# Another order for the query tasks in two steps around layer 1 of a two-layer attention kernel

## The chip, the cores and the metric

One core of a Trainium2 chip runs the whole kernel. The metric is the device time of one launch in microseconds (us). The kernel before takes 2398.43 us, the median of three runs from 2395.92 to 2399.86.

## The reference

The input x is 8 images of 32 x 32 points with 256 channels in 32-bit floats, so 1024 tokens per image. Two layers follow each other.

```python
# layer 0: attention with 4 heads, C = 256 channels per head
qkv = einsum('bnc,cd->bnd', xf, W_qkv)          # q, k, v
atten = softmax(einsum('bihd,bjhd->bijh', q, k) * C ** -0.5, axis=2)
res = einsum('bijh,bjhd->bihd', atten, v).reshape(B, -1, h * C)
x = einsum('bnd,dc->bnc', res, W_out) + b_out + xf
# layer 1: attention with one head, keys and queries of 32 channels
f, g, h = x @ Wf + bf, x @ Wg + bg, x @ Wh + bh
o = einsum('bij,bjd->bid', softmax(einsum('bik,bjk->bij', g, f)), h)
y = gamma * o + x
```

## The kernel before

**Steps.** The work is cut into units and steps. A unit is one head of layer 0 for one image (class `Layer0`) or layer 1 for one image (class `Layer1`). Each unit has two steps, one for each block of 512 of its 1024 query tokens. The list `steps` runs over the images. For every image after the first, layer 1 of the image before is put between its heads 1 and 2, for the last image behind head 3 (`behind`). Layer 1 of the last image comes at the very end. So layer 1 stands between two heads of layer 0 six times.

**What one step holds.** The loop that ends at the edit writes the order out by hand. In it `a` and `blk` are the unit and block of step i, `one` and `two` are the steps one and two before, and `nxt` is the next. A step computes the scores of its own block, the product of the probabilities of `one` with the values, and the output projection of `two`; in the last step of a unit also the queries of the next unit. Each task gets a place, a number, with `put`; the tasks of a step are emitted in the order of these numbers. TensorE, VectorE and ScalarE are scheduled by hand (`manual_schedule`), so this is the order in which these three engines run. A number has no unit; only the order counts.

**Tasks of layer 0.** Its scores, its products and its queries use a scheme with seven block products in place of eight (`seven`, L222). A call makes three tasks and holds three PSUM banks, x, y and z. Task one (L254) writes the three banks; ScalarE copies x to SBUF as e, and VectorE adds y and e to u. Task two (L261) adds products onto x and y; then ScalarE takes x out, and VectorE adds y and e to v and z and v to an output. Task three (L268) adds products onto y and z, and VectorE makes the last two outputs, which frees these banks. Scores make two such calls per step, six tasks, placed at 0, 2, 4, 6, 8 and 10 (L815). Queries and products make one call each. A call for the product has three tasks, of which the third is put into the next step (L823). The scheme needs sums and differences of its operands, on VectorE: four small ones of the queries (`qsums`, L460, L461), four of the probabilities (L526, L529), called s1 to s4 in the order of their making, and per image those of the values and keys.

**Tasks of layer 1.** A scores task (L647) computes four 128 x 512 pieces, each into a PSUM bank of its own. A matmul here uses 32 of the 128 rows, and four lie side by side. ScalarE copies the banks to SBUF (L660). VectorE takes the maximum (L697 to L703), GpSimd makes it one over all partitions (L705), VectorE subtracts (L712) and ScalarE exponentiates (L717), a quarter of the block at a time. A block's product is four tasks (L726), each with a bank of its own for 16 matmuls (each 32-bit float matmul is two in the profile), and VectorE normalises and adds (L738, L740).

**Buffers.** The pool `ps` has six PSUM banks, shared by the scores, the products and the queries. Two more (`psm`) serve projections and transposes.

**The places around the change.** The queries and their sums are placed at L841 to L845:

```python
if is_l0(nxt) and blk == NBLK - 1:
    queries, qsums = nxt[0].queries()
    put(queries, *((1.5, 2.5, 4.5) if not l0 or is_l0(two) else (0.5, 1.5, 4.5)))
    put(qsums, *((5.4, 6.4, 7.2, 7.4) if l0 else (6.7, 6.9, 7.3, 7.6)))
```

In layer 1's second step the scores tasks are at 0.5 and 2 (L818), the softmax pieces at 0.9, 2.7, 4.2, 5, 6.2, 6.8 and 7.5, the products at 1, 4, 6 and 8 (L835) and the projections at 3 and 7 (L825). In a layer 0 step the product of `one` has its two tasks at 5 and 9 (L833), with its sums at 2.2, 3.2, 4.2 and 5.2 (L830, L831). The case `(0.5, 1.5, 4.5)` is a step of layer 0 with no layer 0 step two before it: head 2's second block behind layer 1, six times, and step 1 of the whole run.

Of the kernel before, what the change touches and what calls it, by code (L numbers as in the profile page):

```python
# [20 lines left out]
def kernel(  # L21
# [93 lines left out]
    def load_x(b, parts=1):  # L115
        t = tile_of("rows", [P, NT, C], f"x_{b}")
        n = HT // parts
        for k in range(NBLK):
            for i in range(parts):
                nc.sync.dma_start(  # L120
                    t[:, k * HT + i * n : k * HT + (i + 1) * n, :].rearrange("p t c -> p (t c)"),
                    x_v[b][:, k, ts(i, n * C)],
                )
        rows[b] = t
# [206 lines left out]
    def transpose_rows(b, src, dst, layer):  # L331


        def task(k, c):
            if b not in dst:
                dst[b] = tile_of("xT", [P, CC, N], f"x{layer}T_{b}")
            pt = tile_of("psm", [P, NB], f"px{layer}_{b}_{k}_{c}")
            for t in range(HT):
                nc.tensor.transpose(  # L339
                    pt[:, ts(t, P)], src[b][:, k * HT + t, ts(c, P)], ident  # L340
                )
            nc.scalar.copy(dst[b][:, c, ts(k, NB)], pt)

        return [partial(task, k, c) for k in range(NBLK) for c in range(CC)]

    def key_sums(b):

        made = {}

        def piece(i):  # L350
            if i == 0:
                xT = xT_of[b]
                t = tile_of("v", [P, 4, HN], f"xs_{b}")
                sums = [t[:, k, :] for k in range(4)]
                blocks = [xT[:, c, ts(k, HN)] for k in range(2) for c in range(CC)]
                made["l"] = sum_a(sums, *blocks)
                xblocks[b] = a_operands(blocks, sums)
            made["l"][i]()

        return [partial(piece, i) for i in range(4)]  # L360

    def value_sums(b):

        made = {}

        def piece(i):
            if i == 0:
                r = rows[b]
                t = tile_of("xt", [P, 4, NT // 2, P], f"xt_{b}")
                blocks = [r[:, ts(j, NT // 2), ts(c, P)] for j in range(2) for c in range(CC)]  # L370
                sums = [t[:, k] for k in range(4)]
                made["l"] = sum_b(sums, *blocks)
                vblocks[b] = b_operands(blocks, sums)
            made["l"][i]()

        return [partial(piece, i) for i in range(4)]

    def residual(b):


        def piece(i):
            if i == 0:
                rows1[b] = tile_of("rows", [P, NT, C], f"x1_{b}")
            nc.vector.tensor_tensor(
                rows1[b][:, ts(i, 2), :], rows[b][:, ts(i, 2), :],
                bout_sb.unsqueeze(1).broadcast_to([P, 2, C]), ALU.add,
            )

        return [partial(piece, i) for i in range(NT // 2)]
# [387 lines left out]
    def behind(b):  # L777

        return 2 if b < B - 1 else HEADS
# [10 lines left out]
    queries, qsums = first.queries()  # L790
# [5 lines left out]
    def is_l0(s):  # L796
        return s is not None and isinstance(s[0], Layer0)

    def step(k):
        return steps[k] if 0 <= k < len(steps) else None  # L800
# [4 lines left out]
    for i, (a, blk) in enumerate(steps):  # L805
        l0 = isinstance(a, Layer0)
        one, two, nxt = step(i - 1), step(i - 2), step(i + 1)
        places = []

        def put(tasks, *at):  # L810
            assert len(tasks) == len(at)
            places.extend(zip(at, range(len(places), len(places) + len(at)), tasks))

        if l0:
            put(a.scores(blk), 0, 2, 4, 6, 8, 10)  # L815
        else:
            tasks, pieces = a.scores(blk)
            put(tasks, *((0.5, 2.4) if blk == 0 else (0.5, 2)))  # L818
            put(pieces, *((1.6, 3.9, 6.2, 6.5, 7.4, 8.4, 8.6) if blk == 0 else
                          (0.9, 2.7, 4.2, 5, 6.2, 6.8, 7.5)))  # L820
        if is_l0(two):
            u, k = two
            put(u.products_of[k][2:], 1 if l0 else 0)  # L823
            put([partial(u.invert, k)], 2.9 if l0 or blk == 1 else 1.9)
            put(u.project(k), *((3, 7) if l0 else (2, 6) if blk == 0 else (3, 7)))  # L825
        if is_l0(one):
            u, k = one
            sums, keys = u.sums(k)
            u.products_of[k] = u.products(k)
            put(sums[:2] + sums[3:], *((2.2, 3.2, 4.2) if l0 else (0.8, 2.2, 4.5)))  # L830
            put(sums[2:3], 5.2 if l0 else 5.5)  # L831
            put(keys, *((6.2, 8.2) if l0 else (7.6, 9.6)))
            put(u.products_of[k][:2], *((5, 9) if l0 else (4, 7)))  # L833
        elif one is not None:
            put(one[0].products(one[1]), *((3, 5, 7, 9) if l0 else (1, 4, 6, 8)))  # L835
        if i == 0:
            fold = fold_weights(1) + fold_weights(2) + fold_weights(3)
            put(fold, -2, -1, *[0.9 + 0.6 * n for n in range(len(fold) - 2)])
        if i == 1:
            put([partial(nc.vector.tensor_scalar, bh_sb, bh_sb, gamma_sb, None, ALU.mult)], 8.5)  # L840

        if is_l0(nxt) and blk == NBLK - 1:
            queries, qsums = nxt[0].queries()
            put(queries, *((1.5, 2.5, 4.5) if not l0 or is_l0(two) else (0.5, 1.5, 4.5)))
            put(qsums, *((5.4, 6.4, 7.2, 7.4) if l0 else (6.7, 6.9, 7.3, 7.6)))  # L845

        if l0 and a.h == 0 and blk == 0:
            put(residual(a.b), 5.3, 6.3, 7.3, 7.4)
        if l0 and a.h == 0 and blk == 1:
            put(value_sums(a.b), 1.4, 2.4, 3.4, 4.4)  # L850
        if l0 and a.h == 2 and blk == 0 and a.b + 1 < B:
            load_x(a.b + 1)
        if l0 and a.h == HEADS - 1 and blk == 0 and a.b + 1 < B:
            put(transpose_rows(a.b + 1, rows, xT_of, 0), 1.5, 2.5, 3.5, 4.5)
            put(key_sums(a.b + 1), 5.4, 6.4, 7.2, 7.4)

        if l0 and a.b > 0 and a.h == behind(a.b) - 1:
            if blk == 0:
                put(transpose_rows(a.b - 1, rows1, x1T_of, 1), 2.5, 4.5, 6.5, 8.5)
            else:  # L860
                put(nxt[0].queries(), 1.4, 1.5, 3.5)
        if not l0 and blk == 0:
            put(a.values(), 0.9, 1, 3, 5, 8)
        if nxt is None:
            put(transpose_rows(B - 1, rows1, x1T_of, 1), 8.1, 8.2, 8.3, 8.4)
            put(final.queries(), 9, 9.1, 9.3)
        for _, _, t in sorted(places, key=lambda x: x[:2]):
            t()
# [136 lines left out]
```

## Time and profile before

| | before |
|---|---|
| time, median of 3 (us) | 2398.43 |
| span of the profiled execution (us) | 2399.1 |
| instructions | 25946 |
| DVE busy (us) | 1584.2 |
| ACT busy (us) | 623.7 |
| POOL busy (us) | 236.5 |
| mean granted TensorE clock | 0.997 |

PE is TensorE's matmuls, PEld its weight loads, DVE is VectorE, ACT is ScalarE, POOL is GpSimd. Times in rows are microseconds if not marked ns. A row of the waits reads: engine, what it wrote and the line, `<-` what released it, then the total time in us, how often, and the longest. A row of the timeline reads: start from the beginning of the span, duration, engine, line, operation, output `<-` inputs, how many were merged, and in brackets the idle time before it with its releaser. Ends of matmuls are modelled, starts are recorded. A row of the windows gives the busy time of PE, PEld, DVE, ACT and POOL, then the granted clock as a share of full speed, the DMA share and GB/s. Of the names: psx, psy and psz are banks of layer 0's scores, with `_q` of the queries, with `_y` of the products; ps_l and pa_l are banks of layer 1's scores and products; po is a projection's.

### The profile page before, as it was taken

The page shows a single profiled execution, that of the slowest core. Times are in us where ns is not written, and L with a number is a line of the kernel's source. Part 1 is how long each engine was busy: PE and PEld are TensorE (multiplying, and loading weights), DVE is VectorE, ACT ScalarE, POOL GpSimd, SP SyncE. Part 2 cuts the span into 40 slices and gives each one's busy share as a digit, 9 for nine tenths or more (in the row PEclk, how much of TensorE's full clock was granted, in tenths as well). Part 3 has the DMA queues.
Part 4 walks back from the last instruction along what each step waited for, and adds up shares of the span by engine and source line. Part 5 has one row for each costly group of instructions (what it writes and reads, how often), then busy time and mean ns, then how long its engine had stood idle before and what let it go on. Part 6 is the DMA issues. An engine that isn't in the chain of part 4 may idle for free.

```text
span 2399.1 us, 25946 instructions
## 1 busy us (share of the span) xinstructions
PE 2373.5 (99%) x10608; PEld 1951.4 (81%) x10608; DVE 1584.2 (66%) x2477; ACT 623.7 (26%) x1001; POOL 236.5 (10%) x93
## 2 busy tenths in 40 slices
PE   8999999999999999999999999999999999999999
PEld 6888888788877888788887888878888788888877
DVE  5666777567675676666766667666676666766665
ACT  2222223222232222322223222222222322222232
POOL 0111111011110111101111011110111100011110
PEclk9999999999999999999999999999999999999999
DMA  3000000000000000000000000000000000000000
GB/s 117 1 1 1 1 18 1 18 1 12 7 1 18 1 19 1 1 18 1 18 1 1 18 1 18 1 1 18 1 18 1 1 18 1 1 1 1 1 10 28
DMA packets 43536, 23.63 MB, mean 10 GB/s; under 512 B 36049, under 2 KB 38097, under 8 KB 43409
## 3 DMA queue, kind: packets, MB, share of 16 engines
q1 hardware_dynamic: 43408, 21.90, 3.2%
q8 instruction: 85, 1.39, 0.2%
q14 instruction: 43, 0.34, 0.0%
HBM read 13.37 MB, written 8.52 MB: 9 GB/s over the span
## 4 chain that ended last, share of the span: by engine, by line
PE 96%; DVE 3%; ACT 0%; DMA 0%; issue 0%; SPq 0%; DVEq 0%; ACTq 0%
PE psy L235 14%; PE psy_y L235 13%; PE po L586 9%; PE pa_l L730 9%; PE psx_y L235 9%; PE psz L235 9%; PE psx L235 9%; PE psz_y L235 9%; PE psy_q L235 4%; PE psx_q L235 2%; PE psz_q L235 2%; PE pr_v_l L419 2%; PE ps_l L651 1%; PE px L339 1%; PE pm_fg L399 1%; DVE s_l L712 1%
## 5 line engine op out<-in xcount | busy, mean ns | idle before, releaser
L542 POOL PARTITION_ALL_REDUCE rb<-rs x64 | 206.9, 3233 | 1903.3 <-DVE rs L540 1903.3
L235 PE MATMUL psy<-qs,xs 128*128 128x256 f32 x1024 | 262.9, 379 | 1.3 <-DVE qs L461 1.3
L490 ACT ACTIVATE p<-p 128x1024 f32<-128x1024 f32 x128 | 135.3, 1057 | 492.7 <-DVE p L252 492.7
L235 PE MATMUL psx<-q,x0T 128*128 128x256 f32 x1024 | 262.8, 379 | 0.0
L235 PE MATMUL psz<-q,xs 128*128 128x256 f32 x1024 | 262.8, 379 | 0.0
L586 PE MATMUL po<-wvo,y 128*128 128x256 f32 x1024 | 242.6, 380 | 0.0
L235 PE MATMUL psx_y<-p,x 128*128 128x256 f32 x1024 | 242.0, 379 | 0.0
L235 PE MATMUL psy_y<-s,xt 128*128 128x256 f32 x1024 | 241.9, 379 | 0.0
L730 PE MATMUL pa_l<-v_l,s_l 128*128 128x257 f32 x1024 | 231.7, 381 | 2.3 <-DVE y L252 1.9
L235 PEld LDWEIGHTS psx<-q,x0T 128*128 128x128 f32 x1024 | 193.9, 190 | 39.7 <-issue 15.3
L730 PEld LDWEIGHTS pa_l<-v_l,s_l 128*128 128x128 f32 x1024 | 193.7, 190 | 39.0 <-issue 12.6
L586 PEld LDWEIGHTS po<-wvo,y 128*128 128x128 f32 x1024 | 193.7, 191 | 38.1 <-issue 13.9
L235 PEld LDWEIGHTS psx_y<-p,x 128*128 128x128 f32 x1024 | 192.9, 190 | 36.0 <-issue 12.0
L235 PEld LDWEIGHTS psy<-qs,xs 128*128 128x128 f32 x1024 | 194.5, 190 | 28.1 <-DVE qs L461 1.7
L235 PEld LDWEIGHTS psz<-q,xs 128*128 128x128 f32 x1024 | 194.6, 190 | 26.4
L235 PEld LDWEIGHTS psy_y<-s,xt 128*128 128x128 f32 x1024 | 193.8, 190 | 27.2
L252 DVE TENSOR_TENSOR u<-psy,e 128x512 f32<-128x512 f32 x128 | 88.5, 691 | 155.5 <-PE psy L235 81.1
L264 ACT ACTIVATE p<-psx 128x512 f32<-128x512 f32 x128 | 76.4, 597 | 373.6 <-PE psx L235 373.4
L252 DVE TENSOR_TENSOR v<-psy,e 128x512 f32<-128x512 f32 x128 | 88.1, 688 | 103.4 <-PE psy L235 103.1
L235 PE MATMUL psy<-qs,x0T 128*128 128x256 f32 x512 | 132.1, 380 | 5.5 <-DVE v L252 5.5
L597 DVE SCALAR_TENSOR_TENSOR x<-po,inverse,x 128x256 f32<-128x256 f32 x256 | 111.9, 478 | 25.3 <-PE po L586 15.3
L258 ACT COPY e<-psx 128x512 f32<-128x512 f32 x128 | 73.8, 577 | 206.4 <-PE psx L235 206.4
(108 smaller groups left out, 3164.8 us busy)
## 6 DMA issues: line engine op xcount, KB each, us to landing
out_dram<-x SPq DMA_DIRECT2D x15, 512.0 KB, 2.6
x<-in_x_dram SPq DMA_DIRECT2D x14, 512.0 KB, 4.3
w<-in_L_conv_W_qkv_dram SPq DMA_DIRECT2D x4, 768.0 KB
x<-in_x_dram SPq DMA_DIRECT2D x4, 256.0 KB, 4.5
w<-in_L_conv_W_out_dram SPq DMA_DIRECT2D x4, 256.0 KB, 9.3
line<-rb SPq DMA_DIRECT2D x64, 2.0 KB
st<-line SPq DMA_DIRECT2D x64, 2.0 KB, 2.1
out_dram<-x SPq DMA_DIRECT2D x4, 128.0 KB, 2.2
```

What stands on the lines that cost most here:

```text
L235: nc.tensor.matmul(banks[k][:, ts(i, w)], lhsT=lhsT, rhs=rhs, start=first and n == 0, stop=True, skip_group_check=True,)
L252: nc.vector.tensor_tensor(dst, shaped(banks[k]), shaped(other), ALU.add)
L258: nc.scalar.copy(scratch("e"), banks["x"])
L264: copy(outs["11"](), shaped(banks["x"]))
L339: nc.tensor.transpose(pt[:, ts(t, P)], src[b][:, k * HT + t, ts(c, P)], ident)
L399: nc.tensor.matmul(pm[:m], lhsT=w()[:, c, d * P : d * P + m], rhs=src()[:, c, ts(k, NB)], start=(c == 0), stop=(c == CC - 1),)
L419: nc.tensor.matmul(pm[:, ts(j, C)], lhsT=src()[:, c, ts(2 * t2 + j, P)], rhs=w()[:, c, :], start=(c == 0), stop=(c == CC - 1),)
L490: exp(both, both)
L542: nc.gpsimd.partition_all_reduce(t, r.rearrange("p e i -> p (e i)"), P, bass_isa.ReduceOp.add)
L586: nc.tensor.matmul(pm[:, ts(j, C)], lhsT=self.y[blk][:, c, ts(2 * t2 + j, P)], rhs=folded[self.h][1][:, c, :], start=(c == 0), stop=(c == ...
L597: nc.vector.scalar_tensor_tensor(acc, pm[:, ts(j, C)], inverse[:, n : n + 1], acc, ALU.mult, ALU.add)
L730: nc.tensor.matmul(pm[:, : C + 1], lhsT=p[:, j, ts(ti, P)], rhs=v[:, j, : C + 1], start=(j == 0), stop=(j == NT - 1),)
```

## The change

Three tasks of queries and four sums get other places. In layer 1's second step the queries move behind a product and a projection: the first to behind the second scores task, the second to behind the second product, the third to behind the third product. Two steps behind layer 1 (and in step 1) the second query task moves to between the second and third tasks of scores, the third to behind the first product task, and the sums follow it. The case of `two` in layer 0 stays as it is. No instruction is added or taken away. The aim is that a query task lies between two tasks that use the same banks or each other's results.

```diff
         if is_l0(nxt) and blk == NBLK - 1:
             queries, qsums = nxt[0].queries()
-            put(queries, *((1.5, 2.5, 4.5) if not l0 or is_l0(two) else (0.5, 1.5, 4.5)))
-            put(qsums, *((5.4, 6.4, 7.2, 7.4) if l0 else (6.7, 6.9, 7.3, 7.6)))
+            put(queries, *((2.5, 4.5, 6.5) if not l0 else
+                            (1.5, 2.5, 4.5) if is_l0(two) else (0.5, 2.5, 5.5)))
+            put(qsums, *((6.7, 6.9, 7.3, 7.6) if not l0 else
+                          (5.4, 6.4, 7.2, 7.4) if is_l0(two) else (6.4, 7.2, 7.3, 7.4)))
```

## The prediction

> **What bounds the kernel now.** I read the engine row of the page first, then the chain that ended last:
>
> ```profile
> PE 2373.5 (99%) x10608; PEld 1951.4 (81%) x10608; DVE 1584.2 (66%) x2477; ACT 623.7 (26%) x1001; POOL 236.5 (10%) x93
> ...
> PE 96%; DVE 3%; ACT 0%; DMA 0%; issue 0%; SPq 0%; DVEq 0%; ACTq 0%
> ```
>
> TensorE carries 96% of the chain. The change removes no matmul, so it can only win back time in which TensorE starts nothing, or runs slowly. The view of waits, for TensorE alone, says where that is:
>
> ```profile
> PE psy L235 <- DVE v L252: 5.5, 7, 0.8
> PE px L339 <- DMA x<-in_x_dram: 4.9, 2, 4.0
> PE ps_l L651 <- ACT s_l L660: 4.0, 6, 0.7
> PE pa_l L730 <- DVE y L252: 1.9, 7, 0.3
> ```
>
> The first and third rows occur 7 and 6 times. By the code, the last case of the edit (step B below) is taken seven times, and layer 1's second step (step A) six times. The timeline of TensorE in the first step A shows the third row's wait:
>
> ```profile
> 417.96 3.71 PE L730 MATMUL pa_l<-v_l,s_l 128*128 128x257 f32 x16 [0.27 <-DVE y L252]
> 421.50 1.02 PE L235 MATMUL psx_q<-x0T,wqk 128*128 128x512 f32 x2
> ...
> 424.17 1.13 PE L651 MATMUL ps_l<-fg 32*128 32x512 f32 x6
> 425.97 1.12 PE L651 MATMUL ps_l<-fg 32*128 32x512 f32 x2 [0.66 <-ACT s_l L660]
> 427.02 1.93 PE L235 MATMUL psx_q<-x0T,wqk 128*128 128x512 f32 x2
> ```
>
> Query 1 (421.50) holds three of the six PSUM banks. The second scores task needs four and finds three, so its fourth matmul waits for ScalarE's first copy. The row says 0.66, but the ends of matmuls are modelled; starts are the better measure. The task lasts from 424.17 to 427.02, 2.85 us. A scores task with free banks (391.57 to 392.64 in the timeline) takes 1.07. So 1.78 us are lost here. The timeline in the first full step B:
>
> ```profile
> 478.94 1.03 PE L235 MATMUL psx<-q,x0T 128*128 128x256 f32 x4
> 479.80 1.03 PE L235 MATMUL psy<-qs,xs 128*128 128x256 f32 x4
> 481.61 1.13 PE L235 MATMUL psy<-qs,x0T 128*128 128x256 f32 x4 [0.78 <-DVE v L252]
> ```
>
> Task three of the scores adds onto the bank that VectorE still reads for task two, and no other matmul lies between them. From 479.80 to 481.61 are 1.81 us for matmuls that take 0.86 (478.94 to 479.80): 0.95 lost. Last, the granted clock in windows around the second scores task of two steps A:
>
> ```profile
> 423.00:433.00 10.00, 9.34 (x27) 4.42 (x26) 2.97 (x4) 2.88 (x6) 0.00 (x0) 0.83 0.03 2
> 720.00:730.00 10.00, 9.34 (x36) 5.53 (x35) 4.94 (x6) 2.73 (x5) 0.00 (x0) 1.00 0.02 0
> ```
>
> The column before the last two is the clock. It is 0.83 in three of the six steps A: 3.4 of 10 us at half speed. In the first, query 2's four matmuls run from 427.02 to 430.44 (start of the projection), 3.42 us; in step B they take 1.72 (477.22 to 478.94). Another 1.70 lost.
>
> [...] every window I took around step A's predecessor has clock 1.00. [...]
>
> **Step A (layer 1's second step, six times).** The TensorE order was product 1, query 1, scores 2, query 2, projection 1, product 2, query 3, product 3, projection 2, product 4. It becomes product 1, scores 2, query 1, projection 1, product 2, query 2, product 3, query 3, projection 2, product 4. Prices from starts: query 1 2.58, queries 2 and 3 1.72 each, scores 1.07, projection 1.73, product 3.47. Count from the end of product 1 (421.50). Before, the next step starts at 446.11, so 24.61. After: 1.07+2.58+1.73+3.47+1.72+3.47+1.72+1.73+3.47 = 20.96, if nothing new waits. The 3.65 are the 1.78 and the 1.70, plus 0.17 of small slips that I don't count.
>
> Is anything new waited for? Banks: scores 2 now takes four with only product 1's bank in use. Query 1 takes the sixth free bank, then product 1's (VectorE's two instructions after it end at 0.9, needed at 1.9), then the first scores bank (its copy starts 1.16 after the task, as 416.55 to 417.71, lasts 0.59, so 1.75; needed at 2.8). ScalarE: query 1's copy now stands behind the four scores copies, so it ends at 3.7 and its add on VectorE at 4.5; nothing needs it before query 2 at 8.9. Hidden.
>
> VectorE is the tight queue. Behind that add: second maximum 4.4 to 5.6, then 1.25 and 1.33 later the last maximum, to 7.6; the all-reduce (1.78 us on GpSimd, at 435.38 before, 13.9 after product 1) runs at 7.7 to 9.5. The subtractions wait for it: first 9.7, second behind query 2's adds at 12.2, third behind product 3's two instructions (product 3 ends at 14.0) at 14.9. Then query 3's two adds (16.0 and 16.6, after its matmuls), first sum 17.3, fourth subtraction 17.9, second sum 19.1, projection's adds 19.7, third sum 20.4 to 21.1. The next step's first scores start at 20.96 and use the third sum in their second product at 21.8. Slack 0.7; before it was 0.3 (446.67 to 446.97). The waits don't return: 6 x 1.78 = 10.7 us. The clock: scores 2 is no longer stretched, [...]; 3 x 1.70 = 5.1 us.
>
> **Step B (six behind layer 1, and step 1 of the run).** Order before: scores 1, query 1, query 2, scores 2, scores 3, query 3, product 1. After: scores 1, query 1, scores 2, query 2, scores 3, product 1, query 3. With 2.59 for scores 1, scores 3 starts at 8.6 from the step's start (472.06), and the add it needs (0.69, starts 0.21 after scores 2) ends at 7.8. The 0.95 wait is gone. But product 1 now follows scores 3 at once: its second part (12.06) needs the sum s2 on VectorE. That queue runs: two score adds to 8.5, s1 at 8.4, query 2's adds 9.6 and 10.3, s2 at 10.9 to 12.1. A wait of about 0.1. Its third part (13.8) needs the bank that scores 3's first add frees at 12.7: free. Query 3 before scores 4: its banks are free at 17.4 and 18.3, needed at 18.2 and 19.0. The four query sums, moved from 5.4 to 6.4 and later, push scores 5's add to 24.4, needed at 25.1. Net 0.85, times 6 = 5.1 us. In step 1 the value sums lie in the same queue: two 0.6 slots ahead of what product 1's second part needs, so it waits to 13.4, 1.3 us instead of 0.95. I count 0.3 lost.
>
> Sum: 10.7 + 5.1 + 5.1 - 0.3 = 20.6; 2398.4 - 20.6 = 2377.8, so 2378.
>
> **Bounds of what isn't shown.** The number of slow windows in a timed run: 2395.9 to 2399.9 is a spread of 4.0 us, about two windows' worth, so the median run may hold one or two rather than three: up to 3.4 less gain, 2381. I keep three, as in the profile. Which bank product 1 gets in step B: if its second part gets the bank freed at 12.7, it waits 0.65 rather than 0.1, so 6 x 0.55 = 3.3 less gain, also 2381. Both: 2384. The other way, no wait at all in step B gives 0.9 more; with 2 us of run spread, 2375.
>
> **Rivals.**
> - *Product 1 takes over step B's wait.* For: VectorE's s2 ends when it is needed, and a busier queue eats all of the 0.95. Against: the slot between query 2's adds. Gain 10.7 + 5.1 - 0.3 - (0 to 3) = 12.5 to 15.5, so 2383 to 2386.
> - *Step A's sums come late.* For: 0.7 us slack after a VectorE chain of some twenty instructions. If each of six steps waits 1.5 us at the next step's scores, 9 us are lost again: 2387. Against: the all-reduce comes 6 us earlier.
> - *Slower.* VectorE becomes the bound in A and B: the score banks free later, and waits of 2 us in 13 steps on top of the 20.6 now lost would give 2398.4 - 20.6 + 20.6 + 26 = 2424; past 2403 they must exceed 25 us in all. Against: VectorE is busy 15.8 of 24.6 us in step A and 20.2 of 27.8 in B (windows view).
>
> **How the numbers follow.** Forecast 0.74; product 1's wait 0.14; late sums 0.06; both rivals so large that nothing is left, within 0.2%, 0.03; slower 0.03. The first two and the bounds make the range 2374 to 2387, with late sums at its edge. Faster by over 0.2% (below 2393.6): 0.74 + 0.14 + 0.06 = 0.94. Within: 0.03. Slower: 0.03.
>
> **What would show it.** Right: both rows gone from the waits; second scores tasks of 1.07 us; clock 1.00 in all six steps A; from product 1's end to the next step 21.0. Step B: 26.9 us instead of 27.8. Wrong: a row psy_y waiting for VectorE's s or a bank of more than 0.3 each; psy waiting for qs behind step A; a clock of 0.83 that persists without a wait, [...].

## The result and the profile after

The changed kernel takes 2380.84 us, the median of six runs from 2379.35 to 2382.21. The kernel before took 2399.14 us in its six runs beside it (2395.92 to 2401.07). The ratio is 0.9925, with a 95% interval of 0.9912 to 0.9938: 18.3 us or 0.75% faster. The forecast was 2378, with a range of 2374 to 2387.

The first row of the page after, and then TensorE's waits after (what waited, what released it, us in total, times, longest):

```profile
PE 2361.3 (99%) x10608; PEld 1948.2 (82%) x10608; DVE 1585.2 (67%) x2477; ACT 621.9 (26%) x1001; POOL 236.4 (10%) x93
```

```profile
PE px L339 <- DMA x<-in_x_dram: 5.4, 2, 3.9
PE pa_l L730 <- DVE y L252: 1.9, 7, 0.3
...
PE psy_y L235 <- DVE xt L374: 1.2, 1, 1.2
```

The two rows that the change was aimed at, psy behind VectorE's v and ps_l behind ScalarE's s_l, are gone. Among the steps one row is new: in step 1 of the run, product 1 waits once, 1.2 us, for the value sums on VectorE. The instruction counts of all engines in the row above are those of before. The trace as a whole lists 25958 instructions, 12 more than before: VectorE and ScalarE each have six more waits for a semaphore, which come with the other order.

TensorE's timeline after, in the first step A (layer 1's second step), start and duration in us first:

```profile
418.36 3.71 PE L730 MATMUL pa_l<-v_l,s_l 128*128 128x257 f32 x16 [0.27 <-DVE y L252]
421.99 1.14 PE L651 MATMUL ps_l<-fg 32*128 32x512 f32 x8
423.06 1.13 PE L235 MATMUL psx_q<-x0T,wqk 128*128 128x512 f32 x2
424.02 1.02 PE L235 MATMUL psy_q<-xs,wt 128*128 128x512 f32 x2
...
443.03 1.03 PE L235 MATMUL psx<-q,x0T 128*128 128x256 f32 x4
```

The second scores task is one piece of eight, from 421.99 to 423.06: 1.07 us where it took 2.85. Query 1 follows it without a gap. From the end of product 1 (421.99) to the next step (443.03) are 21.04 us; 20.96 had been worked out. The first full step B (two steps behind layer 1) after:

```profile
474.15 1.03 PE L235 MATMUL psx<-q,x0T 128*128 128x256 f32 x4
475.01 1.03 PE L235 MATMUL psy<-qs,xs 128*128 128x256 f32 x4
475.87 1.02 PE L235 MATMUL psx_q<-x0T,wqk 128*128 128x512 f32 x2
...
477.59 1.03 PE L235 MATMUL psy<-qs,x0T 128*128 128x256 f32 x4
...
479.32 1.89 PE L235 MATMUL psx_y<-p,x 128*128 128x256 f32 x8
481.23 1.97 PE L235 MATMUL psy_y<-s,xt 128*128 128x256 f32 x8
```

Query 2 now fills the place of the wait, and scores 3 starts at 477.59 with none. Product 1's second part starts at 481.23, 1.91 us after its first, where 1.73 is usual: 0.18 lost, where about 0.1 had been worked out. The granted clock (third column from the end) in the windows around two steps A after:

```profile
423.00:433.00 10.00, 10.00 (x40) 6.89 (x37) 6.53 (x11) 3.13 (x6) 1.78 (x1) 1.00 0.03 2
1901.00:1911.00 10.00, 10.00 (x48) 8.79 (x47) 7.23 (x13) 2.27 (x4) 0.00 (x0) 1.00 0.14 54
```

It is 1.00 in all six windows, where three of six had 0.83.

**Where the time went,** from the starts of the same tasks in both traces (spans 2399.1 and 2379.7 us):

| part | forecast, us | traces, us |
|---|---|---|
| step A without the clock: 6 x 1.77 | 10.7 | 10.6 |
| half clock: 3 windows x 1.70 | 5.1 | 5.1 |
| step B: 27.78 to 26.99, 6 x 0.79 | 5.1 | 4.7 |
| step 1: 27.78 to 28.19 | -0.3 | -0.4 |
| one step 0.34 longer, see below | - | -0.3 |
| start and end of the run | - | -0.3 |
| sum | 20.6 | 19.4 |

### The profile page after: what moved, and what is told of

It is laid out like the page before. It is cut to its first block, busy times and chain, and to the rows that moved or that the text cites. A ratio compares the mean times of both kernels' runs of the same rounds, so it can differ in the third digit from the quotient of the medians.

```text
span 2379.7 us, 25958 instructions
## 1 busy us (share of the span) xinstructions
PE 2361.3 (99%) x10608; PEld 1948.2 (82%) x10608; DVE 1585.2 (67%) x2477; ACT 621.9 (26%) x1001; POOL 236.4 (10%) x93
## 4 chain that ended last, share of the span: by engine, by line
PE 96%; DVE 3%; DMA 0%; issue 0%; ACT 0%; SPq 0%; DVEq 0%; ACTq 0%
PE psy L235 14%; PE psy_y L235 14%; PE pa_l L730 9%; PE po L586 9%; PE psx L235 9%; PE psz L235 9%; PE psx_y L235 9%; PE psz_y L235 9%; PE psy_q L235 3%; PE psx_q L235 2%; PE psz_q L235 2%; PE pr_v_l L419 2%; PE pm_fg L399 1%; PE ps_l L651 1%; PE px L339 1%; DVE s_l L712 1%
```

## The experiments

The theory has three parts. In step A the wait is for a PSUM bank, since query 1 holds three. The half clock follows from the scores task that this wait stretches. In step B the wait is between two scores tasks with nothing between them, and query 2 fills it. The rivals: the gain comes from one step alone; what counts in A is VectorE's queue, which would need queries 2 and 3 to move as well; the half clock is chance or comes from the short matmuls as such; the wait in A is for ScalarE's queue.

### The same kernel again, for its spread (e1)

No edit.

> The order of before, unchanged, for the spread of its runs. Theory: [...] so the runs differ by whole windows of about 1.7 us of lost time. Expected: median 2399, runs from 2395 (none or one window) to 2401 (three or four), each run's mean clock lower by 0.0007 per window, and the longer runs those with the lower clock. Rival, plain noise: the same spread with the same clock of all runs.

Its median is 2397.51 us over 13 runs, 1.5 us under the 2399 written down, with a ratio of 0.9997 (0.9989 to 1.0005) to 24 other runs of the kernel before. The 37 runs by their mean clock: three with 0.997, 2401.3 to 2402.0; ten with 0.998, median 2399.0; 23 with 0.999, median 2397.7; one with 1.000, 2397.3. The groups of 0.998 and 0.999 overlap by 1.8 us, so the clock isn't all of the spread, but the order is as expected. Another part comes from the start: in the traces of this document other than e8's, the first scores task begins between 22.24 and 25.10 us, ahead of all tasks that were moved. Its own trace has a mean clock of 0.999, which over 2395.6 us leaves room for at most two stretches of half clock of 3.41 us, not three. One of them is in this step A:

```profile
1898.25 1.13 PE L651 MATMUL ps_l<-fg 32*128 32x512 f32 x6
1900.05 1.12 PE L651 MATMUL ps_l<-fg 32*128 32x512 f32 x2 [0.66 <-ACT s_l L660]
1901.10 1.77 PE L235 MATMUL psx_q<-x0T,wqk 128*128 128x512 f32 x2
1902.66 1.91 PE L235 MATMUL psy_q<-xs,wt 128*128 128x512 f32 x2
```

The two psx_q matmuls take 1.56 us (1901.10 to 1902.66) where 0.86 is usual, and the clock from 1898 to 1908 us is 0.83: about 3.4 of 10 us at half speed.

The trace of before shows how its half-clock stretches lie. Four start in it, at 427.21, 1608.22, 1905.18 and 2396.70 us. The first three last 3.41 us each, the last runs into the end of the span. The times between the starts, 1181.01, 296.96 and 491.52 us, are 346, 87 and 144 times 3.4133. Counted on in both directions from 427.21, this length cuts the trace into windows of 3.41 us. Of the six stretched scores tasks in the trace, those at 424.17, 1605.24 and 1901.78 lie inside one such window (the last by 0.01 us), and half clock starts with the next window each time. Those at 720.71, 1015.55 and 1310.40 cross an edge (the first by 0.05 us), and none is followed by half clock: the clock from 720, 1015 and 1309 us on is 1.00 over 10 us. So in these six cases half clock came after the stretch of 2.85 us only where all of it lay inside one window of 3.41 us. Why, and whether it holds beyond the six, is not shown.

### Step A alone (e2)

```diff
-            put(queries, *((1.5, 2.5, 4.5) if not l0 or is_l0(two) else (0.5, 1.5, 4.5)))
+            put(queries, *((2.5, 4.5, 6.5) if not l0 else
+                            (1.5, 2.5, 4.5) if is_l0(two) else (0.5, 1.5, 4.5)))
```

> Only layer 1's second step (A) gets the new places; two steps behind layer 1 (B) and step 1 stay. Theory: 1.77 us in each of six steps A, and every slow window: 10.7 us + 1.7 us for each of the one to three windows of a run, so 2399.1 - 12.4 to 15.8 = 2383.3 to 2386.7, clock 1.000 in all runs, row ps_l <- ACT gone, row psy <- DVE v still 7 times 0.8. Rival, most of the gain comes from B: 2394 or more.

Measured: 2386.36 us (2385.50 to 2386.61), ratio 0.9949 (0.9935 to 0.9963), 11.8 us less than the 2398.18 beside it. The clock is 1.000 in all five runs. Of its waits:

```profile
PE psy L235 <- DVE v L252: 5.5, 7, 0.8
PE px L339 <- DMA x<-in_x_dram: 5.3, 2, 3.9
PE pa_l L730 <- DVE y L252: 1.9, 7, 0.3
```

Step B's row stays and step A's is gone. A gives about two thirds of the gain. The rival that B gives most of it falls.

### Step B and step 1 alone (e3)

```diff
-            put(queries, *((1.5, 2.5, 4.5) if not l0 or is_l0(two) else (0.5, 1.5, 4.5)))
-            put(qsums, *((5.4, 6.4, 7.2, 7.4) if l0 else (6.7, 6.9, 7.3, 7.6)))
+            put(queries, *((1.5, 2.5, 4.5) if not l0 or is_l0(two) else (0.5, 2.5, 5.5)))
+            put(qsums, *((6.7, 6.9, 7.3, 7.6) if not l0 else
+                          (5.4, 6.4, 7.2, 7.4) if is_l0(two) else (6.4, 7.2, 7.3, 7.4)))
```

> Only step B and step 1 get the new places; A stays. Theory: six times 0.79 gained and 0.41 lost in step 1: 4.3 us, so 2394.8 (2393 to 2397); the row ps_l <- ACT stays 6 times 0.7, and the clock stays below 1.000 in runs that meet a window. Rival, most of the gain comes from B: 2387 or less.

Measured: 2392.97 us (2389.96 to 2397.09, 12 runs), ratio 0.9976 (0.9967 to 0.9984), 5.2 us less, 0.03 under the range written beside the 2394.8. Step B takes 26.98 and step 1 28.19 us, as in the changed kernel, so 4.4 of the 5.2 are theirs. Five runs have a clock of 1.000 (median 2391.1), five 0.999 (2393.3) and two 0.998 (2395.1 and 2397.1). With the waits of A in place, the runs again lie in the order of their clock, over 7 us. The changed kernel's six lie within 2.9. In its trace one window of half clock falls on the last step A:

```profile
1892.00:1902.00 10.00, 9.34 (x24) 3.85 (x23) 2.02 (x4) 3.32 (x6) 0.00 (x0) 0.83 0.03 0
```

### In step A, query 1 alone moved (e4)

```diff
-            put(queries, *((1.5, 2.5, 4.5) if not l0 or is_l0(two) else (0.5, 1.5, 4.5)))
+            put(queries, *((2.2, 2.5, 4.5) if not l0 else
+                            (1.5, 2.5, 4.5) if is_l0(two) else (0.5, 1.5, 4.5)))
```

> The order of before, but in step A query 1 alone moves from before the second scores task to directly behind it (places 2.2, 2.5, 4.5); queries 2 and 3, B and step 1 stay. Theory (banks): the second scores task lasts 1.07 us, the clock is 1.000, the gain is that of A alone but for a wait of 0.1 to 0.3 us of query 2 behind ScalarE's copy of query 1: 2383.5 to 2388. The VectorE queue worked by hand ends its third sum 0.35 us before it is needed. Rival (queries 2 and 3 must move too, as their VectorE work holds up the maximum and the sums come late): row psy <- DVE qs in six steps with 1 us or more each, 2391 or more.

Measured: 2386.34 us (2386.26 to 2387.68), ratio 0.9951 (0.9937 to 0.9964), clock 1.000 in all runs: the same as with all three queries moved. Its timeline:

```profile
421.90 1.14 PE L651 MATMUL ps_l<-fg 32*128 32x512 f32 x8
422.97 1.12 PE L235 MATMUL psx_q<-x0T,wqk 128*128 128x512 f32 x2
...
424.79 1.02 PE L235 MATMUL psz_q<-xs,wt 128*128 128x512 f32 x2
425.65 1.13 PE L235 MATMUL psx_q<-x0T,wqk 128*128 128x512 f32 x2
426.62 1.02 PE L235 MATMUL psy_q<-xs,wt 128*128 128x512 f32 x2
```

The scores task takes 1.07 us. Query 2 at once behind query 1 loses 0.11 (0.97 from 425.65 to 426.62 instead of 0.86), so step A is 0.1 us longer than in e2. No row of psy behind the queries' sums appears beside the single one at the start of the run. Moving queries 2 and 3 further apart, behind the products, brings only this 0.1 per step. The rival of VectorE's queue falls.

### Seven banks instead of another order (e8)

```diff
-        y=2, e=2, u=2, w=1, eh=1, uh=1, st=2, r=8, line=4, ps=6, psm=2,
+        y=2, e=2, u=2, w=1, eh=1, uh=1, st=2, r=8, line=4, ps=7, psm=1,
```

> The order of before, with seven banks in the pool of scores, products and queries and one in that of projections and transposes. Theory (banks): the second scores task of step A finds four free banks, lasts 1.07 us in all six, the row ps_l <- ACT is gone and no window of half clock falls on it; the row psy <- DVE v (7 times 0.8) stays, since it isn't for want of a bank. The whole time isn't compared, because the single other bank brings new waits of px, pr_v, po and pm_fg. Rival (the wait is for ScalarE's queue, not for a bank): ps_l <- ACT stays near 0.7 each.

Its timeline in step A, with query 1 still ahead of the scores:

```profile
449.81 1.02 PE L235 MATMUL psz_q<-xs,wt 128*128 128x512 f32 x2
450.76 1.14 PE L651 MATMUL ps_l<-fg 32*128 32x512 f32 x8
451.83 1.12 PE L235 MATMUL psx_q<-x0T,wqk 128*128 128x512 f32 x2
```

The scores task is whole again, 450.76 to 451.83, 1.07 us, and no wait for ScalarE's copies is left. In step A it was the bank. Step B's row stays at 5.5 us, 7 times: there it isn't. The row of pa_l behind VectorE's y is gone too, and layer 1's second step takes 25.77 us from its first scores to the next step, where the changed kernel takes 26.09. The whole takes 2477.95 us, since the single other bank brings waits of its own:

```profile
PE pm_fg L399 <- DVE x L597: 14.8, 7, 2.1
...
PE psy L235 <- DVE v L252: 5.5, 7, 0.8
```

In the step above no half clock falls on the second scores task or behind it: the query matmuls that follow take 0.97 and 0.85 us (451.83 to 453.65). There is half clock elsewhere, since the mean clock of the run is 0.993. The times of the matmuls show it in the step in which layer 1's queries (pm_fg) wait 2.1 us:

```profile
387.04 1.91 PE L586 MATMUL po<-wvo,y 128*128 128x256 f32 x8
391.06 2.70 PE L399 MATMUL pm_fg<-x1T,wfg_sb 128*128 128x512 f32 x4 [2.11 <-DVE x L597]
393.55 1.91 PE L235 MATMUL psy<-qs,x0T 128*128 128x256 f32 x4
395.26 1.20 PE L235 MATMUL psz<-q,xs 128*128 128x256 f32 x4
```

psy's four take 1.71 us (393.55 to 395.26), twice the usual 0.86. There are no matmuls of 32 rows in this stretch, so here the slow matmuls came behind a wait of 2.11 us without them.

### In step B and step 1, query 2 alone moved (e5, e6)

e5 is the changed kernel once more, on the chip of e6 to e8. e6 is the changed kernel with this edit:

```diff
-                            (1.5, 2.5, 4.5) if is_l0(two) else (0.5, 2.5, 5.5)))
+                            (1.5, 2.5, 4.5) if is_l0(two) else (0.5, 2.5, 4.5)))
...
-                          (5.4, 6.4, 7.2, 7.4) if is_l0(two) else (6.4, 7.2, 7.3, 7.4)))
+                          (5.4, 6.4, 7.2, 7.4)))
```

> The changed kernel itself, on the chip of the next two, to compare with them and with the kernel before once more. Expected 2380.8 (2379 to 2383), clock 1.000 in every run.

> The changed kernel, but in step B and step 1 query 2 alone is moved (places 0.5, 2.5, 4.5) and the sums stay at 5.4, 6.4, 7.2 and 7.4. Theory: query 2 between the scores tasks is what removes the wait of 0.95, and query 3 between scores 3 and product 1 gives VectorE 1.72 us more for the sums, so that product 1 waits neither in step B (0.16 us in the changed kernel) nor in step 1 (1.4 us). Step B 26.83 us instead of 26.99, step 1 26.83 instead of 28.20; 6 x 0.16 + 1.37 = 2.3 us less than the changed kernel, 2378.5 (2377.5 to 2379.5). Rival (query 3 must move too): a new wait of query 3 or product 1, 2381 or more.

e5 takes 2380.97 us (2379.65 to 2381.87); two of its five runs show a clock of 0.999, which I had not expected. One of the two is the run of its trace, which has no row of TensorE's waits that the changed kernel's first trace lacks. Half clock can also come where it costs nothing: in the trace of before the last 2.43 us (2396.71 to 2399.14) have a clock of 0.50 and 0.00 us of matmuls. In a span of 2379.8 us as much would make a mean of 0.99949. So a clock of 0.999 need not stand for a window that cost time; which of the two e5 had is not shown. e6 takes 2378.45 us (2377.94 to 2379.17), 2.5 us less, and the runs of the two don't overlap. By the traces 2.0 us of it are the steps' (6 x 0.20 in step B and 0.80 in step 1); the first scores task also began 0.55 us earlier in e6. Ratios to the kernel before on this chip: 0.9932 (0.9919 to 0.9946) and 0.9922 (0.9909 to 0.9936). Step B is 26.79 us. Step 1 is 27.39, not the 26.83 written down. Its timeline says why:

```profile
62.05 1.03 PE L235 MATMUL psz<-q,xs 128*128 128x256 f32 x4
63.48 1.12 PE L235 MATMUL psy_q<-x0T,wt 128*128 128x512 f32 x2 [0.40 <-DVE v_q L252]
```

Query 3 waits there for VectorE, which works on a value sum first. Still, putting query 3 behind the product cost time in the change: it took the 1.72 us between scores 3 and product 1 from VectorE's sums. (e6 puts the queries' sums back as well, but in both orders they stand behind the sums that product 1 waits for.)

### Product 1 ahead of the scores as well (e7)

To the edit of e6:

```diff
-            put([partial(u.invert, k)], 2.9 if l0 or blk == 1 else 1.9)
-            put(u.project(k), *((3, 7) if l0 else (2, 6) if blk == 0 else (3, 7)))
+            put([partial(u.invert, k)], 2.9 if l0 else 1.4 if blk == 1 else 1.9)
+            put(u.project(k), *((3, 7) if l0 else (2, 6) if blk == 0 else (1.5, 7)))
...
-            put(one[0].products(one[1]), *((3, 5, 7, 9) if l0 else (1, 4, 6, 8)))
+            put(one[0].products(one[1]), *((3, 5, 7, 9) if l0 else (0.4, 4, 6, 8)))
```

> As the kernel with query 2 alone moved in step B, and in layer 1's second step product 1 goes ahead of the first scores task (0.4), the inversion and projection 1 to between the two scores tasks (1.4, 1.5). Theory: product 1 then takes a bank that has long been free, in place of one that VectorE has just read; the row pa_l <- DVE y (7 times 0.27, 0.34 us lost each) goes, 2.4 us less: 2376.1 (2375 to 2377.5). Rival: VectorE, held up at the inversion by the sums' DMA, hands its delay on to the sums of the queries; then a row psy <- DVE qs takes its place and the time is 2378.5 or more.

Measured: 2377.41 us (2375.96 to 2378.73), ratio 0.9917 (0.9904 to 0.9931). The row of pa_l behind y is gone, and the stretch from the start of the last layer 0 step before layer 1 to the start of the first behind it falls from 85.67 (e6) to 85.36 us. Two single waits of px appear at the end of the run:

```profile
PE px L339 <- DVE x L597: 0.6, 1, 0.6
PE px L339 <- ACT x1T L342: 0.5, 1, 0.5
```

So 1.9 us are gained in six such stretches, where 2.4 had been worked out. The step directly behind each layer 1 takes 26.05 us instead of 25.95, which gives back 0.6, and the last layer 1 in the loop is 0.7 us longer. From the first scores task to the start of the last step, 0.6 us remain. The runs of e6 and e7 overlap; the traces tell them apart, the times don't.

### Two tasks moved, nothing else (e9)

```diff
-            put(queries, *((1.5, 2.5, 4.5) if not l0 or is_l0(two) else (0.5, 1.5, 4.5)))
+            put(queries, *((2.2, 2.5, 4.5) if not l0 else
+                            (1.5, 2.5, 4.5) if is_l0(two) else (0.5, 2.5, 4.5)))
```

> The order of before with two tasks moved and nothing else: query 1 to directly behind the second scores task in step A (2.2, 2.5, 4.5), query 2 to between scores 2 and 3 in step B and step 1 (0.5, 2.5, 4.5); the sums stay. Theory (only the task that holds the banks, and the one that stands between, count): step A 85.8 us from first scores to first scores of the next layer 0 step, as with query 1 alone, 26.8 in step B; the gains add up, 10.0 of A, 6 x 0.99 of B, 0.4 to 1.4 of step 1, and the slow windows: 2378 to 2379.5, clock 1.000. Rival (the other moves of the change are needed once both steps are mended): 2381 or more, with rows psy <- DVE qs or psy_y <- DVE s of 0.3 us or more.

Measured: 2377.50 us (2376.77 to 2379.09), ratio 0.9919 (0.9905 to 0.9932) to the 2397.51 beside it, a little under the range written down; one of its five runs shows a clock of 0.999. The stretch over layer 1, as in e7, is 85.78 us, step B 26.79, step 1 27.39. Its longest waits:

```profile
PE px L339 <- DMA x<-in_x_dram: 3.6, 1, 3.6
PE pa_l L730 <- DVE y L252: 1.9, 7, 0.3
PE psy L235 <- DVE qs L461: 1.3, 1, 1.3
PE psy_q L235 <- DVE v_q L252: 1.2, 2, 0.8
```

Both rows of before are gone. The one new wait over 0.3 us among the steps is that of query 3 in step 1, 0.4 us, which e6 has too. The ratio lies below the changed kernel's 0.9925 and 0.9932, but the intervals overlap, and the two weren't run beside each other. By the traces its steps are 1.7 us shorter than the changed kernel's: 6 x 0.20 in step B, 0.80 in step 1 and 0.34 in one more step (see below), less 6 x 0.10 in step A. Its first scores task also began 2.5 us earlier in the trace (22.24 against 24.77); no moved task lies there, so this is no gain of the order. So it does at least as well as the change with two of its moves. e6, e7 and e9 are all versions that beat the kernel before; e6 and e7 also beat the changed kernel beside them.

## Why the prediction was right

**Step A, the bank.** Right, to 0.01 us per step: 1.78 worked out, 1.77 found. That it was a bank is shown from two sides, by e4 (one query moved) and e8 (one bank more).

**Step A, nothing new waits.** Right. The times worked out for VectorE's queue, from the second maximum to the third sum, all lie within 0.2 us of the trace. Its end:

```profile
439.44 0.69 DVE L461 TENSOR_TENSOR qs<-q 128x512 f32<-128x512 f32 x1
440.05 1.22 DVE L712 TENSOR_TENSOR s_l<-s_l,cmax_l 128x1024 f32<-128x1024 f32 x1
441.18 0.69 DVE L461 TENSOR_TENSOR q<-q 128x512 f32<-128x512 f32 x1
441.79 0.87 DVE L597 SCALAR_TENSOR_TENSOR x<-po,inverse,x 128x256 f32<-128x256 f32 x2
442.57 0.68 DVE L461 TENSOR_TENSOR qs<-q 128x512 f32<-128x512 f32 x1
```

The third sum runs from 20.6 to 21.3 us after product 1 (421.99); 20.4 to 21.1 had been worked out. TensorE needs it at 443.89 by the usual 0.86 after 443.03, so 0.6 us of slack are left.

**The half clock.** It went with the waits, as forecast: 1.00 in all six steps A, where three had 0.83. The size was too large for a typical run. I counted three windows, as in the one trace, and named one or two as the other end. By their mean clock of 0.999 the traces of e1 and e3 hold at most two stretches of 3.41 us each, and each shows one in a step A. If it is taken as chance where a task falls among the windows, a task of 2.85 us lies inside one of 3.41 us with a share of (3.41 - 2.85) / 3.41 = 0.16; times six steps A that is one window per run, an estimate from these two times of the trace of before. The profiled run of before, at 2400.94, was 1.8 us over the median 2399.14, about one window.

The gain was 18.3 us where 20.6 had been forecast. The steps alone give 14.6 of it by the traces (10.6 + 4.7 - 0.4 - 0.3), which leaves 3.7, about two windows. The same difference leaves 1.5 us in e2 and 1.8 in e4, about one window. So this term of 5.1 was 1.4 to 3.6 us too large. The other 0.9 of the missing 2.3 are in step A (0.1), step B (0.4), step 1 (0.1) and the longer step (0.3). The rest of the way from 2378 to 2380.84 is the kernel before, whose median was 2399.14 beside the changed one and not 2398.43.

That a scores task without a wait brings no half clock was my expectation, and the six steps A of the changed kernel bear it out. The 3.41 us ahead of the first stretch in the trace of before, 423.80 to 427.21, were not empty: they held a task that takes 1.07 us without a wait and took 2.85, with the last 0.37 us of query 1 ahead of it and the first 0.19 of query 2 behind.

**Step B.** The wait went as forecast, and the new wait of product 1 came where it was worked out: s2 was put at 12.1 us after the step's start, and in the trace it ends at 481.08, 12.1 after 468.98.

```profile
479.87 1.22 DVE L529 TENSOR_TENSOR s<-ss,p 128x1024 f32<-128x1024 f32 x1
481.00 0.68 DVE L252 TENSOR_TENSOR p<-psy,e 128x512 f32<-128x512 f32 x1
```

The first rival, in which this wait eats the gain, had the right place and the wrong size: 0.18, not 0.95. What I did not work out is the cheaper choice: with query 3 left where it was (e6) step B has no such wait at all.

**Step 1.** 0.41 lost where 0.3 was forecast.

**Late sums and slower.** Neither came: the sums end 0.6 us before they are needed, and in steps A and B no wait was added but the 0.18 us of product 1.

**Not foreseen:** one step of layer 0 at 572 us is 0.34 us longer after the change, in e2, e5, e6 and e7 too, and not in e3, e4 and e9. VectorE idles 0.46 us between two of its instructions there, with nothing that the trace shows as released later. It goes with the full move in step A, and with the count of VectorE's semaphore waits: 381 in the five traces that have it, 375 in before, e3, e4 and e9. Whether that is the cause is not shown; it stays open.

## What to carry to other kernels

Where a row of waits has an exact count, look for the place in the code that runs so often; two counts, 6 and 7, led to the two places here. Measure the loss from starts to starts, since the idle time in a row showed 0.66 of 1.78 us and 0.78 of 0.95. In the order written by hand here, the task that holds three banks over its length did better behind than before the task that needs four at once (1.78 us in each step A), and the dependent pair of tasks needed one other task between (0.95 us in each step B); more moves than that can cost again, as that of query 3 did here (0.20 us in each step B, 0.80 in step 1), because each moves other engines' work too.

## What the runs showed of the hardware

- In the trace of before, three stretches of half clock of 3.41 us fell on matmuls; under the first, four matmuls took 3.42 us for 1.72, 1.70 lost. Each came after a stretch of 2.85 us of four 32-row matmul pairs with a bank wait among them, 1.78 us longer than without it. All three of these lay inside one of the windows of 3.41 us counted from the first stretch; the three that crossed an edge were not followed by half clock.
- In e8, matmuls took twice their time (1.71 us for 0.86) behind a wait of 2.11 us, with no 32-row matmul from 385.7 to 397.3 us.
- Scores tasks of the same eight matmuls without a wait, 1.07 us, were not followed by half clock in the six steps A of the changed kernel (clock 1.00 in all six windows), nor in the traces of e2, e4, e6, e7 and e9: their mean clock of 1.000 leaves no room for a stretch of 3.41 us, which would bring it to 0.9993.
